# A selective scan in tiles of 32 channels by 4 states, with the sums of two steps in four column quarters

## The chip, the core and the metric

The kernel runs on one core of a Trainium2 chip. The metric is the device time of one execution in microseconds (us). A core has four compute engines with in-order instruction queues: TensorE (PE in the profile, with its weight loads as PEld), VectorE (DVE), ScalarE (ACT) and GpSimd (POOL). SyncE (SP) here only issues transfers; 16 DMA engines carry them out. SBUF is the on-chip memory of 128 partitions, PSUM the small memory that TensorE writes.

## The reference

An input of 8 images, 64 channels, 64 x 64 pixels in float32 goes through four layers: (0) attention over all 4096 pixels of an image, with the input as query and key, a depthwise 3 x 3 convolution and a residual; (1) two blocks of attention in windows of 8 x 8 pixels, 8 heads, each with an MLP; (2) a convolution with a filter computed for each pixel and channel, then a 1 x 9 convolution; (3) a state-space layer: a selective scan over the pixels in four directions, and a multi-scale block. The scan is what the change is about. For each image, direction k and channel c of 128 there are 16 states n:

```python
def step(h, inp):
    u_t, dt_t, B_t, C_t = inp
    h = h * jnp.exp(dt_t[..., None] * A) + dt_t[..., None] * B_t[:, :, None, :] * u_t[..., None]
    return (h, jnp.einsum('bkcn,bkn->bkc', h, C_t))
```

dt and u are given for each channel and pixel, B and C for each state and pixel, A for each channel and state. The result of a channel is a sum over its 16 states. There are 8 x 4 x 128 x 16 such recurrences of 4096 pixels.

## The kernel before

**Order of the work.** The images are worked in four pairs. `front(p)` is layers 0 to 2 and the sources of the scan for a pair, `scans(p)` the scan, `back(p)` what follows it. `front(0)` runs alone at the start. After that the scan of pair p is the main line, and beside it run, in this order, `back(p - 1)` and `front(p + 1)`, as Python generators that yield an estimated cost; after each step of the scan as much of them is taken as keeps the shares equal. The framework draws the waits between instructions and orders each engine's queue by simulated time, with the program's order as priority. The last pair's scan has only the back of the third pair beside it, and its own back begins while it still runs.

**Units and steps.** A scan is cut into units: one image, one direction, 512 pixels. A pair has 64 units, in all there are 256. `inputs` prepares a unit some steps ahead: it loads the source x, computes dt (L1708 to L1714) and dt * x (L1715) into the tile `one` with 128 channels on 128 partitions, copies them with two transfers into `du` (L1719), and writes the rows of B and C to a DRAM scratch (L1725). A unit has 8 steps, and a step treats two states of all channels. A partition of a step's tile is a channel and a state: 64 channels x 2 states fill the 128 partitions, and two such tiles side by side (j = 0 and 1, one for each half of the channels) make the step. So `du` holds for each half the 64 channels repeated twice.

**One step i** is this, spread over the engines:

- `fetch` loads, from the rows, B three steps ahead and C two steps ahead: one transfer each, two rows repeated 64 times to 128 partitions (L1732, 256 KB), into 4 buffers each.
- `products` on POOL, two steps ahead: `vd` = B x (dt u), 128 x 1024 (L1740).
- `step`: ACT computes exp(A dt) into PSUM twice (L1762, `dad`), DVE scans twice (L1765, into `hd` or in place into `dad`), ACT keeps the last column in `carry` (L1773). Then the state times C goes back into `vd`: on POOL for both tiles (L1776, 128 x 1024) or for one (L1779, 128 x 512), and on DVE for the rest (L1779). In the first three pairs an even step is all POOL's and an odd one half DVE's; during global attention (`dense`) and in the last pair DVE takes more.
- `sums` for the step before: TensorE adds the states of a channel by a matmul with `fold`, a 128 x 64 matrix of zeros and ones (L1791). Each of the two tiles goes to one half of the partitions of `yd` in PSUM, which collects all 8 steps of the unit:

```python
u["y"][self.HALF[j]], lhsT=w["fold"], rhs=st["v"][:, j], start=(i % 8 == 0), stop=(i % 8 == 7)
```

The call stands behind the first C product of the next step (`behind`), which orders it in TensorE's queue and adds no wait of its own. After the last step of a unit DVE adds `yd` to `Y` (L1803 to L1808). `yd` has one buffer, `v` six.

An f32 matmul stands in the trace as two records, one for each of two passes.

**Memory for the rest.** Large tiles of front and back (X, att, VT, XP, H3, XI, XT, X3, F, big) take turns in three slabs of 17.4 KB a partition. Their small work tiles come from pools opened by stage: `w_qx`, `w_e` in window attention (L1399, L1447), `m_h` and `hid` in the MLP, `tap`, `act`, `q2` in layer 2, `yb`, `zb`, `half`, `cv`, `up` in back.

Of the kernel before, what the change touches and what calls it, by code (L numbers as in the profile page):

```python
# [9 lines left out]
F32 = mybir.dt.float32  # L10
# [7 lines left out]
P = 128  # L18
# [7 lines left out]
NTD = L // TD  # L26
LEAD = 24
# [61 lines left out]
def _pack(w):  # L89
# [106 lines left out]
    al = f["A_logs"].reshape(KDIR, 2, 64, NST // 2, 2)  # L196
    put("alogs", al.transpose(2, 4, 0, 3, 1).reshape(P, KDIR, NST))
    put("fold", np.repeat(eye, 2, axis=0))
# [961 lines left out]
class _Direct:  # L1160
# [68 lines left out]

    def memory(self, name, shape=(P, L)):  # L1230
        return self.dram.tile(list(shape), F32, name=name, tag=name)
# [128 lines left out]
    def layer1(self, X):  # L1360
        nc, tc, w, net = self.nc, self.tc, self.w, self.net
        with tc.tile_pool(name="w1n", bufs=2) as wk:
            for c in range(NCH):
                x = X[:, c * CH : (c + 1) * CH]
                pc, sd = self.normed(wk, lambda pc: [(pc, x)], w["cen64"], w["avg64"], net.eps[:, 0:1])
                nc.vector.scalar_tensor_tensor(x, pc, w["pe_g"], sd, ALU.mult, ALU.mult)
                nc.scalar.activation(x, x, AF.Identity, bias=w["pe_b"])
                yield 6
        for i in range(2):
            with tc.tile_pool(name="w1a", bufs=2) as wk:  # L1370
                now = self.window_head(i, 0, X, wk)
                for wy in range(8):

                    def ahead(wy=wy):
                        return self.window_head(i, wy + 1, X, wk) if wy < 7 else None

                    now = yield from self.window_row(i, wy, X, now, ahead, wk)
            with tc.tile_pool(name="w1m", bufs=2) as wk:
                yield from self.mlp(i, X, wk)

    def window_head(self, i, wy, X, wk):
# [17 lines left out]
        qx = wk.tile([P, 8, 4, 64], F32, name="w_qx", tag="w_qx", bufs=1)  # L1399
# [22 lines left out]
    def window_row(self, i, wy, X, now, ahead, wk):  # L1422
# [6 lines left out]
        def scores(x):  # L1429

            es = []
            ss = [self.bank(f"w_s{g}", (P, 2, 4, 64)) for g in range(2)]
            for j in range(2):
                for g in range(2):
                    for im in range(2):
                        rows = slice(64 * im + 32 * g, 64 * im + 32 * g + 32)
                        nc.tensor.matmul(  # L1437
                            ss[g][half[im], j],
                            lhsT=K[rows, 64 * (x + j) : 64 * (x + j) + 64],
                            rhs=qx[rows, x + j],  # L1440
                            start=True,
                            stop=True,
                        )
# [12 lines left out]
            return es  # L1456
# [61 lines left out]
    def mlp(self, i, X, wk):  # L1518
        nc, w, net, half = self.nc, self.w, self.net, self.HALF
        gelus = []  # L1520
        for c in range(NCH):
            x = X[:, c * CH : (c + 1) * CH]
            pc, sd = self.normed(wk, lambda pc: [(pc, x)], w["cen64"], w["avg64"], net.eps[:, 0:1])
            H = wk.tile([P, CH], F32, name="m_h", tag="m_h")
            nc.vector.scalar_tensor_tensor(H, pc, w[f"norm2_g{i}"], sd, ALU.mult, ALU.mult)
            hid = []
            for im in range(2):
                ph = self.bank("ph")
                nc.tensor.matmul(ph, lhsT=w[f"f1w{i}"][half[im], :], rhs=H[half[im]], start=True, stop=True)
                h = wk.tile([P, CH], F32, name="hid", tag="hid", bufs=4)  # L1530
# [9 lines left out]
    def layer2(self, X):  # L1540
# [5 lines left out]
        nr = 2 * TAPS  # L1546
        with tc.tile_pool(name="w2", bufs=2) as wk:
            net.load(wk, (5,))
            cf = net.channel_filters(X, wk, self.pf, "f")
            for c in range(NCH):  # L1550
# [4 lines left out]
                q = wk.tile([P, CH], F32, name="q2", tag="q2")  # L1555
# [13 lines left out]
                for t in range(TAPS):  # L1569
# [4 lines left out]
                    tap = wk.tile([P, 8, 64], F32, name="tap", tag="tap", bufs=3)  # L1574
# [3 lines left out]
                a = wk.tile([P, 8, 72], F32, name="act", tag="act")  # L1578
                nc.vector.memset(a[:, :, 0:4], 0.0)
                nc.vector.memset(a[:, :, 68:72], 0.0)  # L1580
# [78 lines left out]
    def scans(self, p, beside, cost):  # L1659
# [34 lines left out]
        self.sums(n - 1, steps[n - 1])  # L1694
# [4 lines left out]
    def inputs(self, u):  # L1699
# [10 lines left out]
        du = u["du"] = wk.tile([P, 2, 2, TD], F32, name="du", tag="du")  # L1710
# [27 lines left out]
    def products(self, i, st):  # L1738
        v = st["v"] = self.sw.tile([P, 2, TD], F32, name="vd", tag="v", bufs=6)
        self.nc.gpsimd.tensor_tensor(v, self.twice(st["B"]), self.units[i // 8]["du"][:, :, 1], ALU.mult)  # L1740

    def step(self, i, st):
# [16 lines left out]
        for j in range(2):  # L1759
            n = n0 + j  # L1760
            da = self.bank("dad", (P, TD), "da")
            nc.scalar.activation(da, u["du"][:, j, 0], AF.Exp, scale=net.As[:, k, n : n + 1])  # L1762
# [19 lines left out]
    def sums(self, i, st, after=None):  # L1782
# [7 lines left out]
        for j in range(2):  # L1790
            m = nc.tensor.matmul(  # L1791
                u["y"][self.HALF[j]], lhsT=w["fold"], rhs=st["v"][:, j], start=(i % 8 == 0), stop=(i % 8 == 7)
            )
# [18 lines left out]
    def back(self, p):  # L1812
# [26 lines left out]
        big = self.flat("big")  # L1839
        with tc.tile_pool(name="w5", bufs=1) as wk:  # L1840
            prev, n, ups = F, 64, []
            for i in range(1, 4):
                n //= 2
                if i == 1:
                    hf = big[:, 0:2048].rearrange("p (a b) -> p a b", b=n)
                else:
                    hf = wk.tile([P, 2 * n, n], F32, name=f"half{i}", tag=f"half{i}")
# [6 lines left out]
                cv = wk.tile([P, n, n], F32, name=f"cv{i}", tag=f"cv{i}")  # L1854
                net.dwconv(cv, pool, w["mw"][:, i, :], w["mb"][:, i : i + 1], n)
                k = 2**i
                if i == 1:
                    up = big[:, 2048:4096].rearrange("p (a b) -> p a b", b=64)
                else:
                    up = wk.tile([P, n, 64], F32, name=f"up{i}", tag=f"up{i}")  # L1860
# [104 lines left out]
```

## Time and profile before

| what | value |
|---|---|
| runs | 13265.84, 13285.64, 13293.01 us; median 13285.64 |
| profiled execution | 13288.26 us, span of its instructions 13286.5 us |
| busy: PE, DVE, ACT, POOL | 10111.5, 8619.6, 7086.1, 7760.7 us |
| mean granted clock of TensorE | 0.817 of full speed |
| transfers | 1579.99 MB, 119 GB/s on average |
| scan steps | 2048, first products from 2201.3 us to 13149.9 us |

The profile is one execution. In its rows, "L1791 PE MATMUL yd<-vd,pack" is the matmul of line 1791 that reads `vd` and a constant pack (where `fold` lies) and writes `yd`; "x8192 | 3311.3, 782" are its records, the time in which at least one of them ran, and the mean of one in ns. Behind the second bar stands the idle time of the engine just before such instructions, and what ended most of it. A view by stretches gives for A:B in us the busy time of each engine with its instruction count, the granted clock, the busy share of the DMA engines and the rate; it can be restricted to one line. The view of waits gives who waited for whom: total us, times, longest. The large idle time before L1740 is the stretch of 2184 us in which `front(0)` runs and no scan has begun.

### The profile page before, as it was taken

The numbers are of one execution on the slowest core, as the hardware profiler recorded it, in microseconds if no ns is written. First come the engines' busy times: TensorE is split into PE (matmuls) and PEld (weight loads), VectorE is DVE, ScalarE is ACT, GpSimd is POOL, SyncE is SP. The second block draws the span as 40 slices with busy tenths as digits, with TensorE's granted clock in tenths as the row PEclk, the third lists the DMA queues.
The fourth block names the chain that finished last, engine by engine and source line by source line (L and its number), as shares of the span: only waits on it lengthen the run. The fifth ranks groups of instructions, "written<-read, shape, count | busy, mean of one in ns | idle before, by whom it ended". The sixth has DMA issues, their size and how long they took to land. (4 is left out here: it accounts for less than half of the span.)

```text
span 13286.5 us, 142109 instructions
## 1 busy us (share of the span) xinstructions
PE 10111.5 (76%) x46358; PEld 3219.0 (24%) x46358; DVE 8619.6 (65%) x10109; ACT 7086.1 (53%) x15584; POOL 7760.7 (58%) x3875
## 2 busy tenths in 40 slices
PE   9999985777777567987888655997887756665566
PEld 2243421323221112223332111222432211111111
DVE  0121235777777676567676778557666777998997
ACT  5556514565545645665563644665555554554553
POOL 0000003888788684456675677447566777887994
PEclk9999976777787578998888676998788867777787
DMA  0000003444445553333343454334333455665663
GB/s 25 1 1 1 1 14 112 147 151 142 140 150 153 163 161 95 101 117 118 113 122 105 157 160 136 103 101 128 104 112 110 130 168 165 182 183 166 204 201 115
DMA packets 779986, 1579.99 MB, mean 119 GB/s; under 512 B 89312, under 2 KB 89440, under 8 KB 778208
## 3 DMA queue, kind: packets, MB, share of 16 engines
q1 hardware_dynamic: 755040, 1514.49, 37.9%
q10 hardware_dynamic: 24192, 56.32, 1.1%
q8 instruction: 367, 6.01, 0.2%
q14 instruction: 387, 3.17, 0.1%
HBM read 1199.26 MB, written 102.76 MB: 98 GB/s over the span
## 5 line engine op out<-in xcount | busy, mean ns | idle before, releaser
L1740 POOL TENSOR_TENSOR vd<-B,du 128x1024 f32<-128x1024 f32 x2048 | 4818.1, 2366 | 3533.2 <-DMA B<-rows 2362.5
L1791 PE MATMUL yd<-vd,pack 128*64 128x512 f32 x8192 | 3311.3, 782 | 1888.0 <-POOL vd L1776 996.9
L1762 ACT ACTIVATE dad<-du,As 128x512 f32<-128x512 f32 x4096 | 2722.3, 681 | 1059.7 <-DVE hd L1765 658.5
L1765 DVE TENSOR_TENSOR_SCAN hd<-dad,carry,vd 128x512 f32<-128x512 f32 x2166 | 2718.5, 1271 | 702.2 <-ACT dad L1762 412.7
L1776 POOL TENSOR_TENSOR vd<-hd,C 128x1024 f32<-128x1024 f32 x658 | 1553.8, 2361 | 1249.7 <-DVE hd L1765 1034.3
L1765 DVE TENSOR_TENSOR_SCAN dad<-dad,carry,vd 128x512 f32<-128x512 f32 x1418 | 1786.4, 1274 | 90.5 <-ACT dad L1762 66.6
L1779 POOL TENSOR_TENSOR vd<-hd,C 128x512 f32<-128x512 f32 x1154 | 1484.0, 1287 | 600.4 <-DVE hd L1765 564.6
L1791 PEld LDWEIGHTS yd<-vd,pack 128*64 128x64 f32 x8192 | 661.3, 162 | 4084.1 <-POOL vd L1776 1472.5
L1315 ACT ACTIVATE e<-s 128x512 f32<-128x512 f32 x2048 | 1201.0, 591 | 824.9 <-PE s L1309 821.3
L1309 PE MATMUL s<-X 64*128 64x512 f32 x4096 | 1337.4, 645 | 32.3 <-ACT e L1315 24.1
L1301 PE MATMUL po<-e,VT 128*64 128x512 f32 x4096 | 1200.0, 621 | 5.0 <-ACT e L1315 5.0
L1779 DVE TENSOR_TENSOR vd<-dad,C 128x512 f32<-128x512 f32 x1626 | 1078.5, 676 | 49.4 <-ACT carry L1773 47.2
L1773 ACT ACTIVATE carry<-hd 128x1 f32<-128x1 f32 (+1 forms) x1586 | 313.2, 200 | 785.7 <-DVE hd L1765 776.1
L1464 PEld LDWEIGHTS w_av<-vals,w_e 64*64 64x64 f32 x16384 | 614.3, 159 | 240.2 <-issue 110.4
L1464 PE MATMUL w_av<-vals,w_e 64*64 64x9 f32 x16384 | 643.4, 216 | 24.6 <-ACT w_e L1454 24.4
L1773 ACT ACTIVATE carry<-dad 128x1 f32<-128x1 f32 x1422 | 239.6, 169 | 701.9 <-DVE dad L1765 698.8
L1708 PE MATMUL pdd<-xs,xdt 128*128 128x512 f32 x512 | 397.0, 867 | 276.2 <-DMA xs<-xc 101.6
L1449 DVE TENSOR_TENSOR w_e<-w_s,bias 128x512 f32<-128x512 f32 x512 | 330.3, 682 | 417.4 <-PE w_s L1437 417.3
L1309 PEld LDWEIGHTS s<-X 64*128 64x128 f32 x4096 | 368.6, 186 | 925.1 <-issue 785.2
L1454 ACT ACTIVATE w_e<-w_e 128x512 f32<-128x512 f32 x512 | 310.2, 625 | 336.1 <-DVE w_e L1449 226.0
L1765 DVE TENSOR_TENSOR_SCAN hd<-dad,vd 128x512 f32<-128x512 f32 x304 | 362.8, 1212 | 168.6 <-POOL vd L1776 67.8
L1576 PE MATMUL acc<-tap,pack 128*128 128x512 f32 x576 | 381.4, 787 | 91.7 <-DVE tap L1575 89.4
(247 smaller groups left out, 10857.0 us busy)
## 6 DMA issues: line engine op xcount, KB each, us to landing
B<-rows SPq DMA_DIRECT2D x2048, 256.0 KB, 3.5
C<-rows SPq DMA_DIRECT2D x2048, 256.0 KB, 3.4
du<-du SPq DMA_DIRECT2D x512, 512.0 KB, 6.1
xs<-xt SPq DMA_DIRECT2D x128, 256.0 KB, 3.2
xs<-xc SPq DMA_DIRECT2D x128, 256.0 KB, 3.2
xc<-xcv ACTq DMA_DIRECT2D x64, 256.0 KB, 2.6
zs<-z ACTq DMA_DIRECT2D x64, 256.0 KB, 3.1
xt<-XT ACTq DMA_DIRECT2D x32, 512.0 KB, 5.0
```

Of the source, the lines that this page charges most:

```text
L1301: nc.tensor.matmul(po[half[im]], lhsT=VT[:, t, half[im]], rhs=es[im], start=(t == 0), stop=(t == 31))
L1309: nc.tensor.matmul(ss[im], lhsT=at(half[im], t), rhs=X[half[im], jc * CH : (jc + 1) * CH], start=True, stop=True)
L1315: nc.scalar.activation(e, ss[im], AF.Exp, scale=C**-0.5, accum_out=parts[:, im, t, jc : jc + 1])
L1464: nc.tensor.matmul(self.av[half[im], x % 4 + j, h, :], lhsT=es[h // 4][half[im], j, h % 4, :], rhs=V[half[im], x + j, h, :], start=True, s ...
L1708: nc.tensor.matmul(pd, lhsT=net.xdt[:, k, :], rhs=x, start=True, stop=True)
L1740: self.nc.gpsimd.tensor_tensor(v, self.twice(st["B"]), self.units[i // 8]["du"][:, :, 1], ALU.mult)
L1762: nc.scalar.activation(da, u["du"][:, j, 0], AF.Exp, scale=net.As[:, k, n : n + 1])
L1765: nc.vector.tensor_tensor_scan(along(to), along(da), along(v[:, j]), first, ALU.mult, ALU.add)
L1773: nc.scalar.activation(cs, ends, AF.Copy)
L1776: st["w"] = nc.gpsimd.tensor_tensor(v, h, self.twice(CC), ALU.mult)
L1779: m = engine.tensor_tensor(v[:, j], hs[j], CC, ALU.mult)
L1791: m = nc.tensor.matmul(u["y"][self.HALF[j]], lhsT=w["fold"], rhs=st["v"][:, j], start=(i % 8 == 0), stop=(i % 8 == 7))
```

## The change

The tile of a scan step becomes 32 channels x 4 states (`GRP = 4`). A pair of steps, i even and i + 1, now treats four states of all channels: four tiles, one for each quarter of the channels, two to a step. The exponentials, scans and products of a step keep their number and shapes.

- `du` has four groups instead of two, made by four transfers of 512 KB, each from 32 partitions, every row repeated four times. The tile doubles to 16 KB a partition.
- `fetch` runs every second step and loads four rows, each repeated 32 times: 256 KB for B and for C that serve two steps; three buffers instead of four.
- `sums` runs every second step, behind the first C product of the step after the pair, with four matmuls, each into 32 partitions of `yd`; `fold` is 128 x 32. `v` has seven buffers.
- To make room, work tiles of front and back move from their pools into slabs: `wide` in layer 1 (`w_qx`, `w_e`, `m_h`, `hid`), `taps` in layer 2 (`tap`, four buffers instead of three, and two `act` tiles whose borders are cleared once), and `big` in back (`yb`, `zb`, `half`, `cv1`, `up`), which is now taken at the start of back. `q2` has one buffer instead of two.

```diff
+GRP = 4
...
-    al = f["A_logs"].reshape(KDIR, 2, 64, NST // 2, 2)
+    al = f["A_logs"].reshape(KDIR, GRP, P // GRP, NST // GRP, GRP)
     put("alogs", al.transpose(2, 4, 0, 3, 1).reshape(P, KDIR, NST))
-    put("fold", np.repeat(eye, 2, axis=0))
+    put("fold", np.repeat(np.eye(P // GRP, dtype=np.float32), GRP, axis=0))
...
+        self.wide = self.flat("wide")
...
-        qx = wk.tile([P, 8, 4, 64], F32, name="w_qx", tag="w_qx", bufs=1)
+        qx = self.wide[:, 0:2048].rearrange("p (x s q) -> p x s q", x=8, s=4)
...
-                e = wk.tile([P, 2, 4, 64], F32, name="w_e", tag="w_e", bufs=4)
+                e = self.share(self.wide, 4 + self.nth % 4).rearrange("p (j h q) -> p j h q", j=2, h=4)
...
+        taps = self.flat("taps")
+        acts = [taps[:, 2048 + 576 * j : 2624 + 576 * j].rearrange("p (h w) -> p h w", w=72) for j in range(2)]
...
-                    tap = wk.tile([P, 8, 64], F32, name="tap", tag="tap", bufs=3)
+                    tap = self.img(self.share(taps, (TAPS * c + t) % 4))
...
             if i + 3 < n:
-                self.fetch(i + 3, steps[i + 3], 0)
+                self.fetch(i + 3, steps, 0)
             if 0 <= i + 2 < n:
-                self.fetch(i + 2, steps[i + 2], 1)
+                self.fetch(i + 2, steps, 1)
                 self.products(i + 2, steps[i + 2])
             if i >= 0:
                 self.step(i, steps[i])
-                if i:
-                    self.sums(i - 1, steps[i - 1], steps[i]["w"])
+                if i and i % 2 == 0:
+                    self.sums(i - 2, steps, steps[i]["w"])
...
-        du = u["du"] = wk.tile([P, 2, 2, TD], F32, name="du", tag="du")
+        du = u["du"] = wk.tile([P, GRP, 2, TD], F32, name="du", tag="du")
...
-        for g in range(2):
-            src = one[self.HALF[g]].rearrange("c q t -> c (q t)").unsqueeze(1).to_broadcast([64, 2, 2 * TD])
+        m = P // GRP
+        for g in range(GRP):
+            src = one[m * g : m * g + m].rearrange("c q t -> c (q t)").unsqueeze(1).to_broadcast([m, GRP, 2 * TD])
             nc.sync.dma_start(du[:, g].rearrange("p q t -> p (q t)"), src)
...
-    def fetch(self, i, st, s):
-
-        n = NST * s + 2 * (i % 8)
-        t = st["BC"[s]] = self.sw.tile([P, TD], F32, name="BC"[s], tag="BC"[s], bufs=4)
-        row = self.units[i // 8]["rows"][n : n + 2]
-        self.nc.sync.dma_start(t, row.unsqueeze(0).to_broadcast([64, 2, TD]))
+    def fetch(self, i, steps, s):
+
+        if i % 2:
+            return
+        n = NST * s + GRP * (i % 8 // 2)
+        t = steps[i]["BC"[s]] = steps[i + 1]["BC"[s]] = self.sw.tile([P, TD], F32, name="BC"[s], tag="BC"[s], bufs=3)
+        row = self.units[i // 8]["rows"][n : n + GRP]
+        self.nc.sync.dma_start(t, row.unsqueeze(0).to_broadcast([P // GRP, GRP, TD]))
...
-        v = st["v"] = self.sw.tile([P, 2, TD], F32, name="vd", tag="v", bufs=6)
-        self.nc.gpsimd.tensor_tensor(v, self.twice(st["B"]), self.units[i // 8]["du"][:, :, 1], ALU.mult)
+        v = st["v"] = self.sw.tile([P, 2, TD], F32, name="vd", tag="v", bufs=7)
+        g = 2 * (i % 2)
+        self.nc.gpsimd.tensor_tensor(v, self.twice(st["B"]), self.units[i // 8]["du"][:, g : g + 2, 1], ALU.mult)
...
-        for j in range(2):
-            m = nc.tensor.matmul(
-                u["y"][self.HALF[j]], lhsT=w["fold"], rhs=st["v"][:, j], start=(i % 8 == 0), stop=(i % 8 == 7)
-            )
-            if after is not None and j == 0:
-                net.behind(m, after)
-        if i % 8 < 7:
+        m = P // GRP
+        for g in range(GRP):
+            o = nc.tensor.matmul(
+                u["y"][m * g : m * g + m],
+                lhsT=w["fold"],
+                rhs=steps[i + g // 2]["v"][:, g % 2],
+                start=(i % 8 == 0),
+                stop=(i % 8 == 6),
+            )
+            if after is not None and g == 0:
+                net.behind(o, after)
+        if i % 8 < 6:
             return
...
+        big = self.flat("big")
         with tc.tile_pool(name="w4", bufs=2) as wk:
...
-                    y = wk.tile([P, CH], F32, name="yb", tag="yb")
-                    z = wk.tile([P, CH], F32, name="zb", tag="zb")
+                    y = self.share(big, im)
+                    z = self.share(big, 2 + im)
...
```

`share(t, n)` is columns 512 n to 512 n + 511 of a slab.

More of the change, by code (lines that the diff above doesn't have):

```diff
@@ L1228, in img, with share @@
         return t.rearrange("p (h w) -> p h w", w=64)
+    @staticmethod
+    def share(t, n):
+        return t[:, CH * n : CH * n + CH]
     def memory(self, name, shape=(P, L)):
@@ L1368, in layer1 @@
                 yield 6
+        self.wide = self.flat("wide")
         for i in range(2):
+            self.nth = 0
             with tc.tile_pool(name="w1a", bufs=2) as wk:
@@ L1446, in scores @@
                 hs = slice(4 * g, 4 * g + 4)
-                e = wk.tile([P, 2, 4, 64], F32, name="w_e", tag="w_e", bufs=4)
+                e = self.share(self.wide, 4 + self.nth % 4).rearrange("p (j h q) -> p j h q", j=2, h=4)
+                self.nth += 1
                 b = bias[:, 0, hs].unsqueeze(1).to_broadcast([P, 2, 4, 64])
@@ L1523, in mlp @@
             pc, sd = self.normed(wk, lambda pc: [(pc, x)], w["cen64"], w["avg64"], net.eps[:, 0:1])
-            H = wk.tile([P, CH], F32, name="m_h", tag="m_h")
+            H = self.share(self.wide, c % 2)
             nc.vector.scalar_tensor_tensor(H, pc, w[f"norm2_g{i}"], sd, ALU.mult, ALU.mult)
@@ L1529, in mlp @@
                 nc.tensor.matmul(ph, lhsT=w[f"f1w{i}"][half[im], :], rhs=H[half[im]], start=True, stop=True)
-                h = wk.tile([P, CH], F32, name="hid", tag="hid", bufs=4)
+                h = self.share(self.wide, 4 + 2 * (c % 2) + im)
                 g = nc.scalar.activation(h, ph, AF.Gelu, bias=net.bf1[:, i : i + 1])
@@ L1546, in layer2 @@
         nr = 2 * TAPS
+        taps = self.flat("taps")
+        acts = [taps[:, 2048 + 576 * j : 2624 + 576 * j].rearrange("p (h w) -> p h w", w=72) for j in range(2)]
+        for a in acts:
+            nc.vector.memset(a[:, :, 0:4], 0.0)
+            nc.vector.memset(a[:, :, 68:72], 0.0)
         with tc.tile_pool(name="w2", bufs=2) as wk:
@@ L1554, in layer2 @@
                 nc.tensor.matmul(pm, lhsT=net.swc, rhs=x, start=True, stop=True)
-                q = wk.tile([P, CH], F32, name="q2", tag="q2")
+                q = wk.tile([P, CH], F32, name="q2", tag="q2", bufs=1)
                 nc.scalar.activation(q, pm, AF.Square, bias=net.sbc)
@@ L1577, in layer2 @@
                     yield 2.3
-                a = wk.tile([P, 8, 72], F32, name="act", tag="act")
-                nc.vector.memset(a[:, :, 0:4], 0.0)
-                nc.vector.memset(a[:, :, 68:72], 0.0)
+                a = acts[c % 2]
                 t1 = wk.tile([P, 8, 64], F32, name="t1", tag="t1", bufs=1)
@@ L1693, in scans @@
                 self.inputs(self.units[i // 8 + 1])
-        self.sums(n - 1, steps[n - 1])
+        self.sums(n - 2, steps)
         self.run(beside)
@@ L1761, in step @@
             da = self.bank("dad", (P, TD), "da")
-            nc.scalar.activation(da, u["du"][:, j, 0], AF.Exp, scale=net.As[:, k, n : n + 1])
+            nc.scalar.activation(da, u["du"][:, 2 * (i % 2) + j, 0], AF.Exp, scale=net.As[:, k, n : n + 1])
             first = 0.0 if at == 0 else self.carries[:, n : n + 1]
@@ L1780, in step, with sums @@
             st.setdefault("w", m)
-    def sums(self, i, st, after=None):
+    def sums(self, i, steps, after=None):
         nc, w, net = self.nc, self.w, self.net
@@ L1838, in back @@
                 yield 6
-        big = self.flat("big")
         with tc.tile_pool(name="w5", bufs=1) as wk:
@@ L1843, in back @@
                 n //= 2
[L1844 to L1847, printed above, removed]
+                at = (0, 1024, 1536)[i - 1]
+                hf = big[:, at : at + 2 * n * n].rearrange("p (a b) -> p a b", b=n)
                 body = prev[:, 1 : 2 * n + 1, 1 : 2 * n + 1].rearrange("p h (w two) -> p h two w", two=2)
@@ L1853, in back @@
                 nc.vector.tensor_tensor(pool[:, 1 : n + 1, 1 : n + 1], h2[:, :, 0, :], h2[:, :, 1, :], ALU.max)
-                cv = wk.tile([P, n, n], F32, name=f"cv{i}", tag=f"cv{i}")
+                if i == 1:
+                    cv = big[:, 0:1024].rearrange("p (a b) -> p a b", b=n)
+                else:
+                    cv = wk.tile([P, n, n], F32, name=f"cv{i}", tag=f"cv{i}")
                 net.dwconv(cv, pool, w["mw"][:, i, :], w["mb"][:, i : i + 1], n)
                 k = 2**i
[L1857 to L1860, printed above, removed]
+                at = (2048, 0, 1024)[i - 1]
+                up = big[:, at : at + 64 * n].rearrange("p (a b) -> p a b", b=64)
                 nc.scalar.activation(
```

## The prediction

> **What bounds the kernel now.** I read the page first, for the engines, the costliest groups and the transfers.
>
> ```profile
> PE 10111.5 (76%) x46358; PEld 3219.0 (24%) x46358; DVE 8619.6 (65%) x10109; ACT 7086.1 (53%) x15584; POOL 7760.7 (58%) x3875
> ...
> L1740 POOL TENSOR_TENSOR vd<-B,du 128x1024 f32<-128x1024 f32 x2048 | 4818.1, 2366 | 3533.2 <-DMA B<-rows 2362.5
> L1791 PE MATMUL yd<-vd,pack 128*64 128x512 f32 x8192 | 3311.3, 782 | 1888.0 <-POOL vd L1776 996.9
> ...
> B<-rows SPq DMA_DIRECT2D x2048, 256.0 KB, 3.5
> ...
> du<-du SPq DMA_DIRECT2D x512, 512.0 KB, 6.1
> ```
>
> No engine is full over the span, so the stages have different limits. The sums (L1791) are a third of TensorE's busy time, and TensorE idles another 1888 us right before them. Next the busy time by stage:
>
> ```profile
> 2250.00:4200.00 1950.00, 1511.56 (x8503) 543.11 (x8499) 1430.31 (x1608) 1010.67 (x2059) 1638.27 (x801) 0.78 0.49 146
> ...
> 5120.00:5850.00 730.00, 711.88 (x2452) 196.10 (x2452) 368.01 (x400) 481.97 (x1419) 304.41 (x153) 0.98 0.35 103
> 6100.00:7350.00 1250.00, 1046.32 (x7584) 438.83 (x7584) 825.99 (x1043) 651.71 (x1252) 793.80 (x386) 0.85 0.37 113
> 7350.00:8250.00 900.00, 498.77 (x946) 114.69 (x945) 707.27 (x747) 468.08 (x854) 655.90 (x318) 0.66 0.49 151
> ...
> 11250.00:13180.00 1930.00, 1171.95 (x2386) 244.21 (x2382) 1760.57 (x1896) 1001.63 (x2254) 1586.05 (x848) 0.79 0.61 183
> ```
>
> The columns are PE, PEld, DVE, ACT, POOL, clock, DMA share, GB/s. The same stretches, for the sums alone and then for the first product alone (L1740, one for each step):
>
> ```profile
> 5120.00:5850.00 730.00, 116.31 (x408) 32.46 (x408) 0.98 0.35 103
> 6100.00:7350.00 1250.00, 306.67 (x773) 61.44 (x772) 0.85 0.37 113
> ```
>
> ```profile
> 2250.00:4200.00 1950.00, 938.00 (x401) 0.78 0.49 146
> ...
> 5120.00:5850.00 730.00, 240.14 (x102) 0.98 0.35 103
> 6100.00:7350.00 1250.00, 452.27 (x193) 0.85 0.37 113
> ```
>
> Division by the steps gives five kinds of stage. (a) Global attention (5120 to 5850, and 8300 to 9000 with 103 steps): 7.16 us a step, PE 6.98: PE is the limit. (b) Window attention, MLP and layer 2 of the second and third pair (6100 to 7350, and 9250 to 10500 with 192): 6.48 a step, PE 5.42, DVE 4.28, POOL 4.11. (c) The first pair: 4.86 a step, POOL 4.09, PE 3.77. (d) Scan sources, back and the rest: 574 steps at about 5.5, DVE and POOL between 4.0 and 4.5, PE 3.1. (e) The last pair: 483 steps of 4.00, DVE 3.65: DVE is the limit.
>
> In (c) PE also stands still for products, seen by the waits of 2250 to 4200 (one idle stretch shows under weight load and matmul):
>
> ```profile
> PEld yd L1791 <- POOL vd L1776: 408.8, 143, 8.4
> PE yd L1791 <- POOL vd L1776: 270.4, 121, 7.5
> ```
>
> 270.4 over 401 steps is 0.67 us, so PE is busy or held for 4.4 of 4.86. Front matmuls stand behind the held sum. Last the timeline of PE in (a):
>
> ```profile
> 5507.89 1.08 PE L1301 MATMUL po<-e,VT 128*64 128x512 f32 x4
> 5508.80 1.03 PE L1791 MATMUL yd<-vd,pack 128*64 128x512 f32 x4
> 5509.76 1.13 PE L1309 MATMUL s<-X 64*128 64x512 f32 x4
> 5510.81 1.08 PE L1301 MATMUL po<-e,VT 128*64 128x512 f32 x4
> ```
>
> Four records are two f32 matmuls of two passes each, and take 1.03 us, not twice that: the two column halves already run together.
>
> **The sums, part by part.** A pair of steps keeps four matmuls, now in four column quarters, issued together. I take it that they cost one batch of today instead of two; the nearest row is the window scores (L1437, 32x64 tiles), whose records start in fours within 25 ns. Twice today's price if quarters don't overlap is the other end.
>
> (a) 205 steps. A batch holds PE for 0.91 to 0.96 us by the starts above. Quarter columns are a new shape between po (64 columns) and s; po after s starts 1.05 us on, against 0.91 for the sum after po, which has its shape, so I add 0.15. Two batches of 0.95 become one of 1.10: 0.40 us a step saved, 82 us (0 to 115).
>
> (b) 385 steps. The sums cost 1.59 a step, half is 0.8. A held sum costs 0.28 (53.9 us of waits for L1776 over 193 steps); the batch now stands behind the step after, and its last product is an odd step's, half as long (L1779, 1.29 us), so I count 0.2 of it gone. PE's need falls by 1.0, to 4.7 of 6.48, and then the chains between DVE, ACT and PE limit. I credit half: 193 us (0 to 385).
>
> (c) 401 steps, where PE gains as much but POOL keeps its 4.09 us. The last pair shows DVE at 91% of its step; POOL at that share would be at 4.5. I credit 0.25 a step: 100 us (0 to 200).
>
> (d) 574 steps; the hold goes, but DVE and POOL keep their work. 0.15 a step: 86 us (-60 to 184).
>
> (e) DVE keeps scans, products and order: 0.
>
> Gains: 82 + 193 + 100 + 86 = 461 us.
>
> **Clock.** Less PE work costs clock: it is 0.98 where PE is 97% busy, 0.85 at 84%, 0.66 at 55%. With a quarter less sums in (b), 0.85 may become 0.80: 6% of 4.6 us over 385 steps is 104 us if PE still limits; I take 40 (0 to 104). [...]
>
> **Transfers.** B and C go from 4096 copies of 256 KB to 2048, 537 MB less, and the SP queue loses 2048 issues of about 0.53 us. Copies of du go from 512 to 1024 of 512 KB, 268 MB and 512 issues of 0.59 us more. The first is a small help nobody waits for: among steps inside a unit POOL waits little for B. The second lies at the head of each unit. By the packet records of the trace the two copies of a unit occupy the 16 engines for 5.4 us (median); four take 10.8. The first copy is issued when `one` is done; the unit's first product starts 10.4 us (median; 8.3 at the 5th percentile) after it. In three units of four the fetch of B follows du in the same queue (3.3 us after it at the median), so B lands behind 1.2 us of issue and start and 10.8 of packets, about 14 us: 3.5 late, 2.6 over all units. Behind the product in POOL's order stands the step's second product, which frees `hd` for the scan two steps on and releases PE's sum. POOL has 0.8 us (c) to 2.4 (b) free a step, so I pass on a third: 0.87 x 255 = 222 us (0 to 663).
>
> [...]
>
> **Edits with one answer.** As, fold and the channel order change contents, not shapes. Scans, exponentials and products keep counts and forms: no cost. v with 7 buffers: the oldest was freed by a batch at least three steps back, as today. B and C with 3 buffers of two steps hold six steps, against four. y now has two steps for its DVE read before the next unit's batch; today one. 48 of the 64 memsets of 85 ns vanish: 4 us, nothing. q2 with one buffer makes the Square (0.68 us) wait for one matmul a chunk, covered by 9 taps.
>
> **Front tiles in slabs.** Same buffer counts, so the same waits inside a stage. But three slabs are now all held in layer 2 (X, XP, taps) and from the start of back (X3, F, big), so H3 waits for XP or taps, and the first y load for the last slab of the front before: the overlap of one chunk, some 3 to 8 us at seven borders. I take 15 (-5 to 60), hidden only if the scan steps fill it.
>
> **The sum.** The profiled execution took 13288.3 us (span 13286.5 and 1.8 around it), 2.6 above the median. 13288 - 461 + 40 + 222 + 15 = 13104; against the median, 13100.
>
> **Rivals.** *Late du:* the copies delay every unit, and all 2.6 us pass on: 13288 - 461 + 55 + 663 = 13545, slower. It decides once a unit loses more than (461 - 55) / 255 = 1.6 us. For: POOL is above 80% busy in (c) and (e), and DVE has no room in (e). Against: POOL's idle time in (b), and products run two steps ahead. *Quarters in turn:* the batch takes as long as two now; only some 100 us of holds go: 13288 - 100 + 222 + 55 = 13465. Against: the window scores overlap in fours, though over rows. *Everything opens:* PE stops limiting (b), POOL fills in (c), du hides behind two steps: 13288 - (115 + 385 + 200 + 184) + 90 + 40 = 12534 at the end, about 12700 in the middle.
>
> **How the numbers follow.** A measurement of this kernel can tell about 0.2%, 27 us, from no change. The likeliest case, 12850 to 13258, gets 0.40, its time 13100; everything opens (below 12850) 0.20; within 0.2%, by cancelling, 0.07; late du 0.26; quarters in turn 0.07. Faster 0.60, same 0.07, slower 0.33. The range 12600 to 13620 leaves out a tenth on each side.
>
> **What would show it.** Right: sums with 32 columns, 8192 records, union near 1700 us instead of 3311, eight records in 1.1 us in global attention, whose two stages together shrink by some 80 us; L1776 waits of PE below half; pace in (b) below 6.0 us a step. Late du: POOL's wait for B at a unit's first product rises from under 1 us to 2 or more, and (e) gets longer than 4.00 a step. Wrong altogether: union of the sums unchanged, or the time lost in front stages on slab waits.

## The result, and the profile after

| | before | after |
|---|---|---|
| median of four runs | 13289.33 us (13265.84 to 13304.16) | 13596.04 us (13579.81 to 13604.96) |
| ratio | 1 | 1.0232 (95% interval 1.0219 to 1.0245) |
| profiled span, mean granted clock | 13286.5 us, 0.817 | 13597.5 us, 0.767 |

The kernel got slower by 307 us, where the prediction had 185 less. The page of the kernel after, engines, groups and transfers:

```profile
PE 9591.7 (71%) x46358; PEld 3001.2 (22%) x46358; DVE 8638.1 (64%) x10061; ACT 7119.5 (52%) x15600; POOL 7755.5 (57%) x3875
...
L1755 POOL TENSOR_TENSOR vd<-B,du 128x1024 f32<-128x1024 f32 x2048 | 4795.8, 2362 | 3709.5 <-DMA C<-rows 2400.9
...
L1807 PE MATMUL yd<-vd,pack 128*32 128x512 f32 x8192 | 2393.2, 820 | 1259.2 <-POOL vd L1791 512.1
...
du<-du SPq DMA_DIRECT2D x1024, 512.0 KB, 8.9
B<-rows SPq DMA_DIRECT2D x1024, 256.0 KB, 4.1
C<-rows SPq DMA_DIRECT2D x1024, 256.0 KB, 3.3
```

The change does what it says on TensorE: busy time falls by 520 us, the sums' union from 3311 to 2393 us, the idle time before them from 1888 to 1259. DVE, ACT and POOL work as long as before. So the lost time is waiting, and two rows say where: a copy of `du` now lands 8.9 us after its issue (6.1 before), and POOL's idle time before the products with B (L1755) rose by 176 us. The stages, in the columns that the prediction used (PE, PEld, DVE, ACT, POOL, clock, DMA share, GB/s): global attention of the second and of the third pair, window attention to layer 2 of the second pair, and the last pair:

```profile
5195.00:5975.00 780.00, 736.07 (x2536) 177.51 (x2534) 396.41 (x423) 508.72 (x1510) 326.16 (x167) 0.93 0.33 82
8403.00:9183.00 780.00, 734.71 (x2535) 177.01 (x2535) 396.46 (x423) 509.13 (x1510) 325.47 (x166) 0.94 0.33 82
6190.00:7391.00 1201.00, 958.26 (x7492) 421.20 (x7485) 815.23 (x1017) 629.11 (x1211) 785.27 (x383) 0.79 0.39 95
11267.00:13458.00 2191.00, 1120.91 (x2455) 190.43 (x2454) 1832.63 (x1954) 1062.23 (x2370) 1669.92 (x892) 0.69 0.55 138
```

The same pieces of work before (for the first, third and fourth row):

```profile
5151.00:5897.00 746.00, 728.84 (x2514) 192.63 (x2514) 367.79 (x394) 497.26 (x1485) 316.52 (x159) 0.99 0.33 99
6116.00:7313.00 1197.00, 1004.26 (x7465) 426.58 (x7465) 794.55 (x1006) 614.27 (x1179) 756.25 (x368) 0.85 0.37 112
11143.00:13150.00 2007.00, 1216.00 (x2473) 253.34 (x2472) 1829.80 (x1963) 1044.08 (x2365) 1671.90 (x893) 0.79 0.61 185
```

The last pair, in which no front work runs and nothing was to be gained, lost 184 us with unchanged DVE and POOL work: 31.4 us a unit (eight steps) became 34.3. Global attention, where TensorE was the limit, is longer too and no longer keeps its clock (0.93 in the second pair, 0.99 before).

Where the time goes is seen at the head of a unit, its first steps. The one shown is among the longer waits of the last pair, where the median is 3.1 us. The timeline of the SP queue there, kernel after (start, duration, what):

```profile
12612.90 7.73 SPq L1731 DMA_DIRECT2D du<-du  x4
12620.73 2.61 SPq L1746 DMA_DIRECT2D B<-rows  x1
12623.45 2.42 SPq L1746 DMA_DIRECT2D C<-rows  x1
```

and of POOL and DVE at that head; the bracket is the idle time before, and who ended it:

```profile
12617.86 1.27 POOL L1794 TENSOR_TENSOR vd<-hd,C 128x512 f32<-128x512 f32 x1 [0.43 <-DVE hd L1780]
12628.27 6.94 POOL L1755 TENSOR_TENSOR vd<-B,du 128x1024 f32<-128x1024 f32 x3 [9.15 <-DMA B<-rows]
```

```profile
12622.34 1.27 DVE L1794 TENSOR_TENSOR vd<-dad,C 128x512 f32<-128x512 f32 x2
12630.65 1.28 DVE L1780 TENSOR_TENSOR_SCAN hd<-dad,carry,vd 128x512 f32<-128x512 f32 x1 [7.04 <-POOL vd L1755]
```

The head of a unit in the last pair of the kernel before, SP and then POOL:

```profile
12370.22 1.20 SPq L1719 DMA_DIRECT2D du<-du  x2
12371.50 2.23 SPq L1732 DMA_DIRECT2D B<-rows  x1
12373.83 2.28 SPq L1732 DMA_DIRECT2D C<-rows  x1
```

```profile
12376.32 1.27 POOL L1779 TENSOR_TENSOR vd<-hd,C 128x512 f32<-128x512 f32 x1 [0.45 <-DVE hd L1765]
12378.30 6.96 POOL L1740 TENSOR_TENSOR vd<-B,du 128x1024 f32<-128x1024 f32 x3 [0.70 <-DMA B<-rows]
```

Two copies left the queue in 1.2 us before; four take 7.73. The fetch of B stands behind them, goes out 7.8 us after the first copy instead of 1.3, and POOL stands still for 9.15 us instead of 0.70, DVE behind it for 7.04. Over all units (medians, by the issue and packet records of the traces, as are all figures of this kind below): the third issue alone takes 3.9 us and the fourth 2.5, where the first two take 0.55 and 0.60; B goes out 7.85 us after the first copy (3.62 before), and the unit's first product starts 15.5 us after it (10.4 before). POOL's idle time right before the first products of units sums to 831 us, against 261 (3.3 and 1.0 us a unit). Before the other products with B it fell, from 1088 to 690 us: inside a unit the scan waits less than before.

### The profile page after: what moved, and what is told of

Its sections match the earlier page's. It is cut to its first block, busy times and chain, and to the rows that moved or that the text cites. A ratio compares the mean times of both kernels' runs of the same rounds, so it can differ in the third digit from the quotient of the medians.

```text
span 13597.5 us, 138564 instructions
## 1 busy us (share of the span) xinstructions
PE 9591.7 (71%) x46358; PEld 3001.2 (22%) x46358; DVE 8638.1 (64%) x10061; ACT 7119.5 (52%) x15600; POOL 7755.5 (57%) x3875
## 5 line engine op out<-in xcount | busy, mean ns | idle before, releaser
L1755 POOL TENSOR_TENSOR vd<-B,du 128x1024 f32<-128x1024 f32 x2048 | 4795.8, 2362 | 3709.5 <-DMA C<-rows 2400.9
L1807 PE MATMUL yd<-vd,pack 128*32 128x512 f32 x8192 | 2393.2, 820 | 1259.2 <-POOL vd L1791 512.1
L1314 PE MATMUL s<-X 64*128 64x512 f32 x4096 | 1397.2, 662 | 84.3 <-ACT e L1320 84.3
L1719 PE MATMUL pdd<-xs,xdt 128*128 128x512 f32 x512 | 438.7, 953 | 794.0 <-DMA xs<-xt 289.8
L1807 PEld LDWEIGHTS yd<-vd,pack 128*32 128x32 f32 x8192 | 328.7, 125 | 2960.7 <-POOL vd L1794 1108.4
L1472 PE MATMUL w_av<-vals,wide 64*64 64x9 f32 x16384 | 664.9, 218 | 77.9 <-ACT wide L1462 77.6
L1472 PEld LDWEIGHTS w_av<-vals,wide 64*64 64x64 f32 x16384 | 636.6, 164 | 263.1 <-ACT wide L1462 128.9
L1247 PE MATMUL pv<-n_sq,pack 128*128 128x512 f32 x576 | 396.1, 775 | 264.2 <-ACT n_sq L1245 237.9
L1457 DVE TENSOR_TENSOR wide<-w_s,bias 128x512 f32<-128x512 f32 x512 | 329.9, 682 | 381.3 <-PE w_s L1444 380.6
L1462 ACT ACTIVATE wide<-wide 128x512 f32<-128x512 f32 x512 | 310.3, 625 | 333.1 <-DVE wide L1457 214.3
```

What stands on the lines that cost most here:

```text
L1314: nc.tensor.matmul(ss[im], lhsT=at(half[im], t), rhs=X[half[im], jc * CH : (jc + 1) * CH], start=True, stop=True)
L1472: nc.tensor.matmul(self.av[half[im], x % 4 + j, h, :], lhsT=es[h // 4][half[im], j, h % 4, :], rhs=V[half[im], x + j, h, :], start=True, s ...
L1719: nc.tensor.matmul(pd, lhsT=net.xdt[:, k, :], rhs=x, start=True, stop=True)
L1807: o = nc.tensor.matmul(u["y"][m * g : m * g + m], lhsT=w["fold"], rhs=steps[i + g // 2]["v"][:, g % 2], start=(i % 8 == 0), stop=(i % 8 == 6),
```

## The experiments

Theory: the copies at the head of each unit cost the time, and the sums in quarters gain. Against it stood: the quarters gain nothing, the front tiles in slabs cost more than thought, or it is the number of copies and not their kind. All experiments were timed against the kernel before; ratios have 95% intervals.

**Half of the copies.** On the kernel after:

```diff
-        for g in range(GRP):
+        for g in range(2):
             src = one[m * g : m * g + m]...
```

> The changed kernel with only two of the four du copies of a unit (1 MB instead of 2 MB); all steps read these two groups, so two channel quarters get the values of the other two. All other instructions keep number and shape. Late du: the burst of du packets falls from 12.8 us to about 6, the first product of a unit starts some 10.5 us after the first copy instead of 15.5, and the time falls to 12900 to 13150 us, below the kernel before, since the sums keep their gain. Colder clock or batched sums as the cause: 13500 to 13600, the copies being hidden. Slabs as the cause: the same 13500 to 13600.

13177.76 us, ratio 0.9909 (0.9892 to 0.9925), just above the range for late copies. All steps read the two groups that are left, so two quarters of the channels are computed with the values of the other two. Two copies less take 418 us off; the first product is back at 10.4 us after the first copy, and POOL's idle time before first products at 390 us. The kernel's loss sits in its four copies. The remaining two move 137 GB/s (1.05 MB in a packet burst of 7.65 us, where about 6 was expected), against 195 GB/s in the kernel before (5.37 us). What differs between them is the source: each of these reads 32 partitions side by side, every row four times, and those of before read 64, every row twice.

**All four copies, other source partitions.** On the kernel after, the channels of `one` are laid out so that each quarter lies on every fourth partition (the weights of `pdd` permuted, x loaded once more in that order, 256 KB a unit); the same bytes, the same four copies:

```diff
-            src = one[m * g : m * g + m].rearrange(...)
+            src = one[g::GRP].rearrange(...)
```

> The changed kernel with its four du copies and all bytes, but each copy reads every fourth partition of the source tile (32 partitions over the whole range) instead of 32 adjacent ones; the rows of the source tile stand in that order, for which x is loaded once more for each unit (256 KB). Late du, with the crowding of the 32 adjacent source partitions as half of it: the burst falls from 12.8 us to 5 to 7, time 12950 to 13200. Late du by bytes alone: burst stays above 10 us, time 13500 to 13650. Colder clock, batched sums or slabs: burst may fall, but time stays at 13500 or more.

13056.61 us, ratio 0.9824 (0.9806 to 0.9842): 540 us less than after, and faster than before. The burst of four copies falls from 12.8 us to 6.0, though the number of packets and bytes is the same; the copies' median 4 KB packet goes from 213 to 162 ns, the 95th percentile from 696 to 241. The transfers of its page and its stages, rows as above (global attention and window attention of the second pair, the last pair):

```profile
du<-du SPq DMA_DIRECT2D x1024, 512.0 KB, 4.6
B<-rows SPq DMA_DIRECT2D x1024, 256.0 KB, 3.4
```

```profile
5015.00:5737.00 722.00, 701.74 (x2537) 172.49 (x2537) 394.82 (x423) 507.80 (x1510) 326.77 (x167) 1.00 0.28 94
5945.00:7131.00 1186.00, 965.55 (x7492) 431.50 (x7485) 814.32 (x1017) 628.66 (x1211) 785.27 (x383) 0.79 0.31 102
10875.00:12898.00 2023.00, 1144.29 (x2460) 198.22 (x2458) 1823.98 (x1955) 1059.71 (x2373) 1675.32 (x892) 0.76 0.47 158
```

Global attention goes 746, 780, 722 us for before, after and this kernel, and its clock 0.99, 0.93, 1.00: the clock was lost to the stalls at the heads of units, not to the shorter sums. The longest idle stretch of TensorE there is 1.80 us before, 7.25 after and 1.87 here. So what matters is which partitions a copy reads, not that there are four. With the new order a row also stands close to the partitions that it is copied to (row 4c + g goes to 4c to 4c + 3); whether the spread or this nearness makes the copies fast, no run tells.

**Front tiles alone.** The scan of before with the slabs of after.

> The kernel before with only the work tiles of front and back moved into slabs; the scan is that of before. Slabs as the cause: 13400 or more. Late du, colder clock or batched sums as the cause: 13290, within 40 us.

13321.58 us, ratio 1.0020 (1.0011 to 1.0030): 31 us dearer. A real but small part.

**The copies alone.** That kernel with two more copies of 32 adjacent partitions at each head, into room that nothing reads:

```diff
+        for g in range(2):
+            src = one[m * g : m * g + m].rearrange(...)
+            nc.sync.dma_start(du[:, 2 + g].rearrange("p q t -> p (q t)"), src)
```

> The kernel before, front tiles in slabs, with two more du copies for each unit (32 adjacent source partitions, 512 KB each, as in the change) behind the two that it needs; nobody reads them. Late du: the fetches behind them in the queue land late, first product 4 to 7 us later after the first copy, time 13290 plus 300 to 900. Colder clock, batched sums: 13290, within 60 us.

13614.58 us, ratio 1.0241 (1.0218 to 1.0264): 293 us above the one without them, on a scan whose sums are untouched. Its first product starts 15.4 us after the first copy, as in the kernel after. So two more copies are enough to make a loss of the size of the change's 307 us. They are not the whole price of the four: nobody waits for the two added ones themselves, and the two that are waited for read 64 partitions, as before. In its view of waits (who waited for whom: us, times, longest)

```profile
POOL vd L1755 <- DMA B<-rows: 2496.2, 77, 2194.3
```

2194.3 us is the front before the first scan, and the rest is 302 us, where the kernel before has 178.

**Spread copies before.** The kernel before with `one[g::2]` in place of its two halves.

> The kernel before (64 channels x 2 states, sums of each step) with its two du copies each reading every second partition of the source tile instead of 64 adjacent ones, x loaded once more for each unit (256 KB). It tells how much of the 1.8% of the changed kernel with spread copies is the copies alone. If the gain there comes from the fewer and shorter sums: 13250 to 13300 here, since the copies of before are mostly hidden. If it is a faster head of the unit: 13050 to 13150 here, burst of du below 3.5 us.

13201.67 us, ratio 0.9941 (0.9925 to 0.9958), between the two ranges that were expected. Its burst takes 3.2 us instead of 5.4, and a copy lands 3.9 us after its issue instead of 6.1: the kernel before already paid 86 us for the same thing. It also gives the base for the sums: with spread copies and slabs, but nothing of the quarters, 13202 + 31 = 13233 (a sum of two differences, no run of its own).

**The last two copies behind B.** On the kernel after, the copies of quarters 2 and 3 are issued three steps before the unit's own steps begin, behind its first fetch of B:

```diff
+            if i >= 0 and i % 8 == 5 and i // 8 + 1 < len(self.units):
+                self.copies(self.units[i // 8 + 1], (2, 3))
```

> The changed kernel with the same four copies of 32 adjacent partitions, but the last two are put into the queue behind the fetch of the next unit's first B, which they delayed. Late du, by way of the fetch of B behind it: first product 10 to 12 us after the first copy, time 13050 to 13250. Late du by the copies' own landing: the second step's product waits instead, 13450 or more. Colder clock, batched sums, slabs: 13550 to 13650.

13316.65 us, ratio 1.0020 (1.0010 to 1.0031), between the two ranges: 280 of the 540 us come back. The first product is at 10.4 us, as before, but the second, which needs quarters 2 and 3, now waits: 315 us in all before second products, where the kernel before has 13. The view of waits has the new one beside the old:

```profile
POOL vd L1763 <- DMA B<-rows: 305.7, 117, 20.5
...
POOL vd L1763 <- DMA du<-du: 263.3, 141, 4.4
```

The place of the copies in the queue is half of the loss; while they are slow, the other half only moves.

**Sums at each step.** The kernel with spread copies, with each step's two matmuls issued at once into its two quarters.

```diff
-                if i and i % 2 == 0:
-                    self.sums(i - 2, steps, steps[i]["w"])
+                if i:
+                    self.sums(i - 1, steps, steps[i]["w"])
```

> The changed kernel with spread copies (e2), but the sums of each step are issued by themselves, into two of the four quarters, one step after it as in the kernel before. If the shorter use of TensorE by four quarters at once and the rarer hold make the gain: 13200 to 13350, busy time of the sums above 3000 us. If the gain over the kernel before comes from half the transfers of B and C or from the copies: 13030 to 13100 as with the sums of two steps together.

13340.62 us, ratio 1.0035 (1.0020 to 1.0049): 284 us slower than with four quarters at once, and 108 above the 13233 of the base. The row of the sums on its page

```profile
L1810 PE MATMUL yd<-vd,pack 128*32 128x512 f32 x8192 | 3083.2, 791 | 2188.0 <-POOL vd L1794 1226.1
```

has 3083 us and 2188 us of idle time before them. With spread copies and joint sums it is

```profile
L1810 PE MATMUL yd<-vd,pack 128*32 128x512 f32 x8192 | 2377.3, 786 | 979.4 <-POOL vd L1794 382.1
```

The joint sums are what gains in this change.

**Inputs a step earlier.** The kernel with spread copies, with the inputs of the next unit at its step 0 in place of 1.

> The changed kernel with spread copies (e2), with the work for the next unit (load of x, dt, copies) called one step earlier, in step 0 of a unit instead of step 1. If the head of a unit still limits: 12850 to 13000, first product of a unit later after the first copy than 12 us and its waits fewer. If other chains limit by now: 13040, within 40 us; if the load of x then blocks the SP queue for its buffer: above 13080.

13032.17 us, ratio 0.9807 (0.9791 to 0.9824). POOL's idle time before first products goes from 110 to 53 us, but before second products from 19 to 78, so the two together stay as they were. The gain, 24 us, is within the intervals of the two.

**Joint sums in halves.** The kernel before with spread copies and slabs; the sums of two steps issued together, but into column halves as before, `v` with seven buffers:

```diff
-                if i:
-                    self.sums(i - 1, ...)
+                if i and i % 2 == 0:
+                    self.sums(i - 2, ...)
+                    self.sums(i - 1, ...)
```

> The kernel before with spread copies (e5) and front tiles in slabs (e3), and the sums of two steps issued together behind the step after them, still 64 channels x 2 states in two column halves; v has seven buffers. Without the pairing this would be 13202 + 31 = 13233 by e5 and e3. If the gain of the quarters is that TensorE is no longer held for the product of the step just before: 13050 to 13130, hold before the sums near 1000 us. If it is the shorter use of TensorE by four quarters at once: 13200 to 13260, busy time of the sums about 3300 us.

13250.53 us, ratio 0.9980 (0.9967 to 0.9994), 17 us above the base of 13233. The row

```profile
L1807 PE MATMUL yd<-vd,pack 128*64 128x512 f32 x8192 | 2984.9, 750 | 1014.6 <-POOL vd L1795 448.5
```

shows that later sums do halve TensorE's idle time before them (1866 us in the kernel before with spread copies), and that in sum this buys nothing. The busy time, 2985 us, is below the 3300 that was expected. By stage it is not nothing (stages cut at the same instructions in every trace; the kernel before with spread copies, then this one):

| stage, us | spread before | joint sums in halves | spread copies, four quarters |
|---|---|---|---|
| global attention | 1503 | 1556 | 1449 |
| window, MLP, layer 2 | 2369 | 2317 | 2341 |
| first pair | 2518 | 2450 | 2430 |
| rest of pairs 2 and 3 | 2465 | 2506 | 2442 |
| last pair | 1986 | 2062 | 2024 |

Of the step from the first column to the second, the slabs make 8, 15, 1, 18 and 0 us, by the run with the front tiles alone. So the later, joint sums gain in the second and third stage and lose as much in the others; why they lose there was not tested. What four quarters at once add shows most in global attention, 107 us between the last two columns (which differ in the fetches and the bytes of `du` too). So the gain needs both: joint sums without four quarters give none in all, nor do four quarters without joint sums.

**Half of the spread copies.** The kernel with spread copies, only two of the four.

> The changed kernel with spread copies, and only two of the four (1 MB for each unit); all steps read these two groups, so two channel quarters get the values of the other two. It tells what the second megabyte still costs when it is copied fast. If the head of a unit still limits: 12900 to 12980, burst near 3 us. If other chains limit: 13020 to 13060.

12966.45 us, ratio 0.9773 (0.9746 to 0.9800): the second megabyte of `du` costs 90 us even when it is fast. Here too, two quarters of the channels are computed with the values of the other two. If it costs the same without joint sums, it is most of the 108 us that the rest of the change cost in the run with sums at each step.

**The copies from ScalarE's queue.** The kernel with spread copies, with `nc.scalar.dma_start` for them.

> The changed kernel with spread copies, issued by ScalarE's queue instead of SP's: the fetches of B no longer stand behind them in one queue, but ScalarE issues four transfers a unit. If the fetch of B behind the copies limits: 12920 to 13020. If ScalarE's order limits (an issue takes some 0.6 us and stands between the exponentials): 13080 to 13250.

13478.40 us, ratio 1.0148 (1.0121 to 1.0175): 422 us worse, worse than either theory had it. ScalarE's timeline at one head:

```profile
12618.66 4.12 ACTq L1734 DMA_DIRECT2D du<-du  x4
12622.83 0.20 ACT L1791 ACTIVATE carry<-hd 128x1 f32<-128x1 f32 x1 [3.49 <-DVE hd L1783]
```

The four issues take 4.12 us, and ScalarE, whose exponentials feed the scans, does nothing for 3.49 us of them. At this head the scan that it waits for next (`hd`) ends only as the issues do, so it is not shown that they cost time here. Over the run there are 914 us of issue time on ScalarE's queue, and only 188 instructions of ScalarE start in the 256 stretches from first to fourth issue. Its view of waits names a second cost:

```profile
POOL vd L1758 <- DMA du<-du: 310.3, 93, 8.3
```

The copies leave later: the first product starts 7.0 us after the first copy, where with SP's queue it is 12.0, and POOL's idle time before first products is 444 us against 110. How the 422 us divide between the two was not shown.

**Both together.** Spread copies, the inputs a step earlier, and the last two copies behind B.

> Spread copies, the work for the next unit one step earlier (e8), and the last two copies behind the fetch of the next unit's first B. If the fetch of B at the head of a unit still limits: 12930 to 13010, below e8. If other chains limit: 13030, within 30 us.

12976.42 us, ratio 0.9768 (0.9741 to 0.9795): this version beats both kernels, 620 us below the one after and 308 below the one before in its own comparison. POOL's waits at heads are not where it gains: before first and second products it idles 132 us in all, against 129 with spread copies alone. Its gain over that kernel is largest in window attention to layer 2 of pairs 2 and 3, 2245 against 2341 us; why was not taken apart. Its page:

```profile
PE 9534.6 (73%) x46358; PEld 3003.1 (23%) x46358; DVE 8655.0 (67%) x10061; ACT 7098.4 (55%) x15602; POOL 7762.3 (60%) x3875
...
du<-du SPq DMA_DIRECT2D x1024, 512.0 KB, 4.1
```

## Why the prediction was wrong, point by point

The time lies inside the range, but the likeliest case had the wrong sign; what came is the rival *Late du*, at 13596 for its 13545. The prediction's sum was 13288 - 461 + 40 + 222 + 15 = 13104. The kernel with spread copies stands in for "copies as short as before" (its burst takes 6.0 us, that of before 5.4), so the error splits in two: without the transfers the sum was 12882, and the chip gave 13057, 175 more; for the transfers it had 222, and the chip gave 13596 - 13057 = 539, 317 more. 175 + 317 is the whole 492. The stand-in is a little better than "as short as before", since POOL idles 110 us before first products in it and 261 before the change; so the split is approximate. That *Late du* came within 51 us is partly luck: it had the gains 175 us too large and the loss 124 too large (663 for 539).

The paces came from round windows: 7.16 us a step in (a) is its first stretch with some of the stage before it, and 4.00 in (e) runs past the last product. Over the whole stages it is 6.95 and 3.93.

**Transfers: the step that failed.** The term was 222 us and measured 539. It had three factors, and each was low.
- *The burst.* "... the two copies of a unit occupy the 16 engines for 5.4 us (median); four take 10.8." They take 12.8, since a copy of 32 adjacent partitions is slower per byte: 164 GB/s in the kernel after and 137 with two of them, against 195 for 64 adjacent ones. That four copies of 32 rows cost no more per byte than two of 64 was the author's estimate behind the 10.8; no run shows it.
- *The queue.* It had B landing behind "1.2 us of issue and start and 10.8 of packets", as if issues cost 0.55 us however many stand ahead (of the other 2 us of its 14 it does not say what they are). The third and fourth issue take 3.9 and 2.5 us, so B isn't merely behind the packets: it isn't issued for 7.85 us. The first product came at 15.5 us and not at 14, 5.1 us later than before and not 2.6.
- *What is passed on.* A third was assumed; 539 / 255 = 2.1 us of 5.1 a unit is 41%. Against the kernel with spread copies, from which the 539 are counted and whose first product starts 12.0 us after the first copy, it is 2.1 of 3.5, or 60%. *Late du* was to decide once a unit loses more than 1.6 us, and that is what happened. Its signs came: POOL's wait at heads up from 261 to 831 us in all, and the last pair from 3.93 to 4.29 us a step.

Which of delay and share failed more depends on that base. But the delay alone was enough: with 5.1 us and the assumed third, the term is already 434, and the sum 13316, slower than before.

By source partition the copies ran at 137 to 164 GB/s from 32 adjacent ones, at 195 from 64 adjacent ones, and at 324 to 351 with rows spread over all 128 (in four of the kernels with them). The prediction priced neither difference, and the second is the larger. The rates were measured; their cause was not shown.

**The gains: right in kind, too large.** Steps of the kernel with spread copies against before, in us:

| stage | before | after | spread copies | saved a step | predicted |
|---|---|---|---|---|---|
| (a) global attention | 6.95 | 7.16 | 6.65 | 0.30 | 0.40 |
| (b) window, MLP, layer 2 | 6.57 | 6.33 | 6.21 | 0.36 | 0.50 |
| (c) first pair | 4.95 | 5.03 | 4.76 | 0.19 | 0.25 |
| (d) rest of pairs 2 and 3 | 5.62 | 5.85 | 5.69 | -0.07 | 0.15 |
| (e) last pair | 3.93 | 4.29 | 3.96 | -0.03 | 0 |

(a) to (c) gained about three quarters of what was credited to a step. (d) was to gain 86 us from the hold alone, and a step there got 0.07 us dearer. Part of that is that steps moved: (b) has 380 where it had 366, (d) 426 where it had 442. In time, (b) is 44 us shorter and (d) 61, so for the same work the two gained 105 us of the 279 credited. In (d) a shorter hold was worth nothing even in halves (2465 to 2506 us, 18 of it slabs), though TensorE waited half as long over the whole run; in (b) it was worth some 67. These columns also hold the 86 us that spread copies gain without any change of the sums. By the base of 13233 the gain is 176 us, where the prediction, less its 40 for the clock, had 421.

**Quarters at once: right.** In global attention a batch costs one batch of before; the timeline of TensorE, kernel after:

```profile
5481.72 1.06 PE L1807 MATMUL yd<-vd,pack 128*32 128x512 f32 x8
5482.71 1.07 PE L1306 MATMUL po<-e,VT 128*64 128x512 f32 x2
```

Eight records take 1.06 us, four of before took 1.03. *Quarters in turn* is out. The union of the sums, though, was to be near 1700 us and is 2393: it halved in (a) and nearly in (b), but in the last pair it went only from 906 to 824. There a batch comes apart: from the first start to the last end of its eight records it takes 3.9 us at the median (1.07 in (a)), with TensorE idle in between for products of POOL and DVE, and a record takes 1059 ns at the median, at a mean granted clock of 0.69 (604 ns at 0.93 in (a)). Hardly anyone waits for these sums, 41 us in the whole last pair.

**Clock: right where it was priced.** In (b) it was to be 0.80 and is 0.79, in both kernels; what that cost in time no run tells. Elsewhere the kernel after has, as means over a stretch, 0.69 in the last pair with TensorE 51% busy, and 0.93 in global attention with its stalls at heads, where the kernel with spread copies has 1.00. Not foreseen was that stalls of the scan would cost the clock of the front.

**Slabs: 15 predicted, 31 measured**, inside its -5 to 60.

The account, each part from a difference of medians: 13288, spread copies on the scan of before -86, slabs +31, sums in four quarters with half the fetches of B and C and twice the bytes of (fast) `du` -176; then the same four copies from 32 adjacent partitions +539, together 13596. Within the -176, joint sums are -284 and the rest +108. How much of the rest is a gain from fewer fetches stays open. The parts depend on the order in which they are taken: with the slow copies already there (13615, the run with the copies alone), all the rest of the change brings 18 us. While the heads are held, little of what the sums save reaches the time.

## What to carry to other kernels

When a change multiplies small transfers ahead of something that is waited for, cost the queue and not only the bytes: here the issue of the third 512 KB copy took 3.9 us at the median and that of the fourth 2.5, and B, which stands behind them, wasn't issued until 7.85 us after the first. Price a copy by a row that reads the same partitions; where there is none, take the slow end as the likely one, and try spreading its rows over all partitions, which here was worth 540 us without moving one byte less. And a shorter wait in the profile's rows is not yet a gain: price it by stage. Here, with the sums in halves, it gained in two stages and lost as much in the others.

## What the runs showed of the hardware

- SBUF to SBUF copies that repeat each row, 512 KB each: 137 to 164 GB/s from 32 adjacent partitions, 195 from 64 adjacent ones, 324 to 351 from 32 or 64 spread evenly over 128. Their 4 KB packets, median and 95th percentile: 213 and 696 ns with four copies from 32 adjacent partitions, 329 and 701 with two of them, 312 and 387 from 64 adjacent ones, 162 and 241 with spread rows.
- Issues of such copies on one queue: 0.55, 0.60, 3.9 and 2.5 us (medians, one after the other), and with spread rows 0.55, 0.60, 0.85 and 1.34. Why the third and fourth take longer was not shown. On ScalarE's queue the four take 0.53, 0.62, 1.02 and 1.39 us.
- Four 128 x 32 float32 matmuls in four column quarters take together about as long as two of 128 x 64, when their inputs are there: 1.06 us in eight records, against 1.03 in four (global attention).
- Mean granted clock in global attention, with the longest idle stretch of TensorE: 0.99 and 1.80 us before, 1.00 and 1.87 with spread copies, 0.96 and 2.55 with joint sums in halves, 0.93 and 7.25 in the kernel after (second pair of each).
